# Three fused last layers: where the sparsemax threshold is subtracted, where int8 values are rounded, and in which step each piece runs

## The chip, the core and the metric

The kernel runs on one core of one Trainium2 chip. The metric is the time of the whole program on the device, in microseconds (us). The core has five instruction streams that matter here: TensorE (PE in the profile; PEld are its weight loads), VectorE (DVE), ScalarE (ACT), GpSimd (POOL) and SyncE (SP, which issues most DMAs). TensorE writes its products into PSUM banks; the other engines read them from there, except GpSimd, which in this kernel works on SBUF tiles only.

## What is computed

The program runs a stack of twelve layers over `x` (32 x 128 x 128). The change touches the last three, which the kernel calls `layer9`, `layer10` and `layer11`:

```python
# layer 9: 16 heads of width 8 attend to 32 patterns, with sparsemax in place of softmax
def sparsemax(z):
    z_sorted = -jnp.sort(-z, axis=-1)
    cum = jnp.cumsum(z_sorted, axis=-1)
    k = jnp.arange(1, S + 1, dtype=z.dtype)
    support = 1.0 + k * z_sorted > cum
    k_sup = jnp.sum(support, axis=-1, keepdims=True)
    tau = (jnp.take_along_axis(cum, k_sup - 1, axis=-1) - 1.0) / k_sup
    return jnp.maximum(z - tau, 0.0)
A = sparsemax(scale * scores)
x = x + (einsum('bhls,bshd->blhd', A, values).reshape(B, L, H * D) @ Wo + bo)

# layer 10: softmax attention to a context, probabilities times a dropout mask
# layer 11: each row scaled by its largest absolute value / 127, rounded to int8,
#           multiplied by int8 weights, scaled back, plus a bias
x_scale = jnp.maximum(amax, EPS) / 127.0
x_q = jnp.clip(jnp.round(x2d / x_scale), -128, 127).astype(jnp.int8)
```

Every layer is preceded by a layer norm and adds its result to `x`.

## The kernel before

The 4096 rows of `x` stay in SBUF as eight groups of 512 rows (`G` = 8), each a tile of 128 partitions by `J` = 4 blocks by 128 columns. The last three layers run as one software pipeline in `layer9` (line 1928).

**What a group goes through.** `scores` norms a group, projects it and puts its 128 x 2048 scores z (4 blocks x 16 heads x 32 patterns) into a `gbig` tile. `sort` sorts each run of 32 scores in 15 stages; a stage is two VectorE instructions (a max and a min) on tiles called `bbig`, and ten of the stages have two ScalarE copies of the elements that the stage leaves alone. `attend` works on four chunks c of 128 columns (4 heads each). `turn_top(c)` turns the sorted scores over on TensorE and ScalarE moves them to SBUF. `lower(c)` makes the candidate thresholds by products with the constant `means`; VectorE takes the largest as `tau`, and GpSimd subtracts it from z in place. `turn_z(c)` turns z over by four TensorE transposes into a `ps` bank, from which ScalarE takes max(z, 0) (a Relu) to SBUF; `value(c)` multiplies that by the value matrix `vb` into 32 rows of an `acc` bank. Then the result is turned back, projected and added. `layer10` and `layer11` follow, each a generator whose `yield`s cut it into steps.

**What sets the order.** Line 2087 builds a schedule by hand: rounds i = 0 to 10 of 15 slots n = 0 to 14. In slot n of round i comes stage n of the sort of group i, and then one step each of `layer11` (group i - 3), `attend` (group i - 1), `layer10` (groups i - 2 and i - 1), `scores` (group i + 1) and `layer11` (group i - 2), in that order, where the numbers behind the name list slot n. In the first slots pieces of the layer before are mixed in.

`follow(T, A, V)` forces TensorE, ScalarE and VectorE to run their instructions in exactly the order in which the program names them, for rounds 0 to 7. So within these engines an instruction that waits holds up all that stands behind it. GpSimd and the DMA queue are ordered by the tile scheduler, and so are all engines in the three last rounds, after `follow()`, where nothing is sorted any more; these are called the tail below.

The buffers that the change concerns: two PSUM banks `ps`, two `acc`, five SBUF tiles `bmid`, ten `gmid`, and four small tiles of 4 x 4 numbers for `tau`. In `layer11`, `E` is GpSimd for groups 0 to 6 and VectorE for group 7.

Of the kernel before, what the change touches and what calls it, by code (L numbers as in the profile page):

```python
# [11 lines left out]
BF16 = mybir.dt.bfloat16  # L12
# [3 lines left out]
ALU = mybir.AluOpType  # L16
AX = mybir.AxisListType
# [7 lines left out]
J = 4  # L25
# [5 lines left out]
class Columns:  # L31
# [5 lines left out]
    def add(self, name, a):  # L37
        a = np.asarray(a)
        assert a.ndim == 2 and a.shape[0] <= 128, (name, a.shape)
        self.at[name] = (a.shape[0], self.n, a.shape[1])  # L40
        self.parts.append(a)
        self.n += a.shape[1]
# [161 lines left out]
def program(ctx, tc, cols, x, ctxt, mask, drop, dfirst, dsmall, dwide, drows, dunits, dexperts, dconst, drel, dwq, out):  # L204
# [29 lines left out]
    def gmid(shape=(128, 512), dtype=F32):  # L234
        return mid.tile(list(shape), dtype, tag="gmid", name="gmid", bufs=10)

    def bmid(shape=(128, 512)):
        return mid.tile(list(shape), F32, tag="bmid", name="bmid", bufs=5)
# [19 lines left out]
    def bc(ap, axis, n):  # L258

        ap = ap.unsqueeze(axis)  # L260
        shape = list(ap.shape)
        shape[axis] = n
        return ap.to_broadcast(shape)
# [1664 lines left out]
    def layer9():  # L1928
# [55 lines left out]

        def attend(i):

            z, top, sTs, aTs = zs[i], ordered[i], {}, {}

            def turn_top(c):
                t = ps()  # L1990
                for j in range(J):
                    T.transpose(t[:, j * 128 : (j + 1) * 128], top[:, j * 512 + c * 128 : j * 512 + c * 128 + 128], ident)
                sTs[c] = bmid()
                A.activation(sTs[c], t, AF.Identity, bias=K["minus"])

            def lower(c):
                tau, m, sT = small(J, 4), acc((128, J, 4, 32)), sTs.pop(c)
                for j in range(J):
                    mm(m[:, j].rearrange("p h k -> p (h k)"), sT[:, j * 128 : (j + 1) * 128], K["means"])
                V.tensor_reduce(tau, m, AX.X, ALU.max)  # L2000
                part = z[:, :, c * 128 : c * 128 + 128].rearrange("p j (h k) -> p j h k", k=32)
                P.tensor_tensor(part, part, bc(tau, 3, 32), ALU.subtract)

            def turn_z(c):
                t = ps()
                for j in range(J):
                    T.transpose(t[:, j * 128 : (j + 1) * 128], z[:, j, c * 128 : (c + 1) * 128], ident)
                aTs[c] = bmid()
                A.activation(aTs[c], t, AF.Relu)

            def value(c):
                mm(yT_ps[32 * c : 32 * c + 32, :], vb[:, c].rearrange("p h e -> p (h e)"), aTs.pop(c))

            turn_top(0)
            turn_top(1)
            yield
            lower(0)
            lower(1)
            turn_top(2)
            yield  # L2020
            lower(2)
            turn_top(3)
            yield
            lower(3)
            turn_z(0)
            yield
            yT_ps = acc()
            for c in range(3):
                value(c)
                turn_z(c + 1)  # L2030
                yield
            value(3)
            yT = gmid()
            A.copy(yT, yT_ps)
            yield

            by = yT.rearrange("p (n l) -> p l n", l=16)
            rows = gbig((32, 16, 16, 8))
            for c in range(0, 4, 2):
                t = two((32, 8, 128))  # L2040
                for n in range(8):
                    T.transpose(t[:, n, :], by[:, 4 * c + n, :], ident)
                A.copy(rows[:, :, 4 * c : 4 * c + 8, :], t.rearrange("p l (h e) -> p h l e", h=16))
                yield
            t = ps((128, 16, J, 8))
            for h in range(16):
                T.transpose(t[:, h].rearrange("p j l -> p (j l)"), rows[:, h].rearrange("p l e -> p (l e)"), ident[0:32, 0:32])
            yT = gmid((128, J, 16, 8))
            for j in range(J):
                A.copy(yT[:, j], t[:, :, j])  # L2050
            yield
            zs.pop(i), ordered.pop(i)
            project(i, yT.rearrange("p j h l -> p (j h l)"), W["a3_Wo"], None)
            yield
# [33 lines left out]
        for i in range(G + 3):  # L2088
            for n in range(15):
                todo = []  # L2090
                add = lambda f, g, *at: todo.extend((f, g) for a in at if a == n and 0 <= g < G)
                add(layer11, i - 3, 0)
                add(attend, i - 1, 0, 1, 2, 3, 4, 5, 6, 7, 8, 9, 10, 11)
                add(layer10, i - 2, 0, 1, 2, 3, 5, 6, 7)
                add(layer10, i - 1, 12, 14)
                add(scores, i + 1, 4, 6, 7, 8, 11, 12)
                add(layer11, i - 2, 8, 10, 11, 12, 14)
                schedule.append((i, n, todo))
        for slot, (i, n, todo) in enumerate(schedule):
            if slot == G * 15:  # L2100
# [29 lines left out]
    def layer10(i):  # L2130

        E = P if i < G - 1 else V
        c, dm = load_ctx(i), gmid((128, J, D))
        SY.dma_start(out=dm, in_=drop[i * J : i * J + J].rearrange("b q k -> q b k"))
        steps = norm_turned(i, WW["L3_xattn_bout"])
        next(steps)
        yield
        next(steps)
        yield
        xnT = next(steps)  # L2140
        yield
        s = ps((128, J, 128))
        for j in range(J):
            cols_j = slice(j * 128, (j + 1) * 128)
            mm(s[:, j, :], xnT[:, cols_j], ctxT[i][:, cols_j])
        m, den, rec = small(J), small(J), small(J)
        pr = bmid((128, J, 128))
        V.tensor_reduce(m, s, AX.X, ALU.max)
        V.tensor_scalar(m, m, -1.0 / 32, None, ALU.mult)
        yield  # L2150
        for half in range(2):
            for j in (2 * half, 2 * half + 1):
                A.activation(pr[:, j], s[:, j], AF.Exp, bias=m[:, j : j + 1], scale=1.0 / 32, accum_out=den[:, j : j + 1])
            if half == 1:
                E.tensor_tensor(pr, pr, dm, ALU.mult)
                V.reciprocal(rec, den)
            yield
        prT = bmid()
        transposed(pr, prT, A.copy)
        yield  # L2160
        o = ps()
        for j in range(J):
            cols_j = slice(j * 128, (j + 1) * 128)
            mm(o[:, cols_j], c[:, j, :], prT[:, cols_j])
        yT = gmid()
        A.copy(yT, o)
        yield
        p = ps((128, J, 128))
        for j in range(J):
            mm(p[:, j, :], yT[:, j * 128 : (j + 1) * 128], W["x3_W"])  # L2170
        for j in range(J):
            V.scalar_tensor_tensor(xg[i][:, j, :], p[:, j, :], rec[:, j : j + 1], xg[i][:, j, :], ALU.mult, ALU.add)
        yield


    def layer11(i):

        rnd = 1.5 * 2.0**23
        E = P if i < G - 1 else V
        xn = mid.tile([128, J, D], F32, tag="xn", name="xn", bufs=2)  # L2180
        steps = norm_act(xg[i], xn)
        next(steps)
        yield
        next(steps)
        P.tensor_tensor(xg[i], xg[i], bc(WW["qbias"], 1, J), ALU.add)
        yield
        am, inv = small(J), small(J)
        V.tensor_reduce(am, xn, AX.X, ALU.max, apply_absolute_value=True)
        V.tensor_scalar(am, am, 1e-6, 1.0 / 127.0, ALU.max, ALU.mult)
        V.reciprocal(inv, am)  # L2190
        yield
        q, qb = bmid((128, J, D)), gmid((128, J, D), BF16)
        for j in range(J):
            A.mul(q[:, j, :], xn[:, j, :], inv[:, j : j + 1])
        E.tensor_scalar(q, q, 127.0, -128.0, ALU.min, ALU.max)
        E.tensor_scalar(qb, q, rnd, rnd, ALU.add, ALU.subtract)
        yield
        t = ps((128, 512), BF16)
        for j in range(J):
            T.transpose(t[:, j * 128 : (j + 1) * 128], qb[:, j, :], identb)  # L2200
        qT = gmid((128, 512), BF16)
        A.copy(qT, t)
        yield
        p = ps((128, J, 128))
        o = bmid((128, J, D))
        for j in range(J):
            mm(p[:, j, :], qT[:, j * 128 : (j + 1) * 128], wq)
        for j in range(J):
            V.scalar_tensor_tensor(o[:, j, :], p[:, j, :], am[:, j : j + 1], WW["qscale"], ALU.mult, ALU.mult)
        V.tensor_tensor(xg[i], xg[i], o, ALU.add)  # L2210
        SY.dma_start(out=out[i * J : i * J + J].rearrange("b s d -> s b d"), in_=xg[i])
        yield
# [52 lines left out]
```

## Time and profile before

| | |
|---|---|
| time, median of 3 runs | 2817.82 us (2806.86 to 2824.95) |
| the profiled execution: its time, its span | 2813.02 us, 2811.2 us |
| busy: PE, DVE, ACT, POOL | 87%, 74%, 54%, 33% of the span |
| mean granted TensorE clock | 0.939 of full speed |

All operations are recorded by one helper, so nearly all carry the line L192; instructions are told apart by the names of what they write and read. `bbig<-bbig` on DVE is the sort; `gbig<-gbig,s` on POOL the subtraction of the threshold; `ps<-cs,gbig` with 128*128 on PE the turning over of z; `bmid<-ps` on ACT the Relu; `acc<-bmid,vb` on PE the value product; `gmid<-bmid` on POOL the rounding.

A PE row gives as 128*32 the weights' rows and columns, then the shape of what streams past them. A float32 product is recorded as two instructions; a float32 transpose as one.

The rounds can be found by the first stage of each sort, the only one that reads a `gbig` tile. Rounds 0 to 7 begin at 2350.2, 2403.2, 2454.6, 2508.7, 2556.6, 2604.4, 2652.0 and 2699.7 us, and the last sort ends at 2744.0. So rounds 3 to 6, in which all three layers run and nothing of the layer before is left, take 47.6 to 47.9 us each, and the tail from 2744 to the end 67 us.

### The profile page before, as it was taken

How to read it: one execution, taken by the hardware profiler on the slowest of the kernel's cores; microseconds unless marked ns; L12 is line 12 of the kernel's file. 1: busy time of each engine (PE TensorE's matmuls, PEld its weight loads, DVE VectorE, ACT ScalarE, POOL GpSimd, SP SyncE). 2: the span in 40 equal slices, each digit the busy share in tenths (PEclk: the TensorE clock that was granted, in tenths of full speed). 3: DMA queues.
4: the chain of work that ended last, by engine and by line, in shares of the span. 5: the costliest groups of instructions: out<-in, count | busy, mean ns of one | idle time of the engine just before them, and what ended most of it. 6: DMA issues, size and time to landing. Idle time of an engine off the chain costs nothing.

```text
span 2811.2 us, 56423 instructions
## 1 busy us (share of the span) xinstructions
PE 2449.9 (87%) x22993; PEld 1590.9 (57%) x23012; DVE 2076.9 (74%) x4091; ACT 1512.4 (54%) x3394; POOL 931.5 (33%) x969
## 2 busy tenths in 40 slices
PE   5998989999979999999997999988878999867664
PEld 3666667777744446666663444445555588444443
DVE  6898768878888858788886454557897525889993
ACT  4665544444412247777773444457885324556663
POOL 3454442322301123445541000133441354243432
PEclk8898899999999999999999999999999999988886
DMA  3000000000000010000000000000002358000000
GB/s 119 2 3 2 6 21 9 9 5 4 14 12 0 1 34 2 6 10 13 10 2 16 1 0 1 1 1 1 2 13 78 103 187 258 16 23 12 23 12 19
DMA packets 51045, 73.77 MB, mean 26 GB/s; under 512 B 3905, under 2 KB 41538, under 8 KB 50658
## 3 DMA queue, kind: packets, MB, share of 16 engines
q1 hardware_dynamic: 47728, 61.63, 7.0%
q0 software_dynamic: 2624, 5.40, 0.5%
q8 instruction: 181, 2.97, 0.4%
q10 hardware_dynamic: 434, 3.14, 0.3%
q14 instruction: 78, 0.64, 0.1%
HBM read 57.26 MB, written 12.89 MB: 25 GB/s over the span
## 4 chain that ended last, share of the span: by engine, by line
PE 55%; DVE 28%; ACT 8%; issue 3%; POOL 2%; DMA 2%; SPq 0%; DVEq 0%; ACTq 0%; POOLq 0%
PE ps L192 23%; PE two L192 17%; PE acc L192 15%; DVE bbig L192 11%; DVE s L192 8%; ACT bbig L192 4%; DVE gmid L192 4%; DVE bmid L192 3%; ACT bmid L192 1%; POOL xn L192 1%; ACT gmid L192 1%; DMA ys<-yt,at 1%; DVE x L192 1%; ACT xn L192 1%; POOL s L192 1%
## 5 line engine op out<-in xcount | busy, mean ns | idle before, releaser
L192 PE MATMUL ps<-cs,bbig 128*128 128x128 f32 x2208 | 334.4, 289 | 86.2 <-ACT bbig L192 32.8
L192 PEld LDWEIGHTS ps<-cs,bbig 128*128 128x128 f32 x2208 | 248.7, 145 | 198.1 <-ACT bbig L192 94.5
L192 ACT COPY bbig<-ps 128x512 f32<-128x512 f32 x418 | 227.2, 583 | 187.1 <-PE ps L192 186.9
L192 DVE TENSOR_REDUCE s<-two 128x8 f32<-128x1024 f32 (+1 forms) x192 | 234.1, 1220 | 72.7 <-PE two L192 71.5
L192 PE MATMUL two<-xnT,u 128*128 128x512 f32 x512 | 262.4, 614 | 12.1 <-ACT bmid L192 5.5
L192 DVE TENSOR_TENSOR bbig<-bbig 128x1024 f32<-128x1024 f32 (+3 forms) x234 | 248.0, 1100 | 9.4 <-ACT bbig L192 7.7
L192 PE MATMUL acc<-bmid,u 128*128 128x512 f32 x416 | 220.2, 616 | 10.2 <-DVE bmid L192 8.9
L192 DVE TENSOR_TENSOR bmid<-bmid,ps 128x512 f32<-128x512 f32 x192 | 130.0, 683 | 114.2 <-ACT bmid L192 94.7
L192 ACT ACTIVATE bbig<-two,s 128x256 f32<-128x256 f32 (+1 forms) x512 | 189.8, 419 | 21.2 <-DVE s L192 17.5
L192 POOL TENSOR_SCALAR gbig<-bmid,cs 128x512 f32<-128x512 f32 x96 | 148.5, 1563 | 149.4 <-ACT bmid L192 149.3
L192 PE MATMUL two<-gbig,gmid 32*128 32x512 f32 (+1 forms) x1248 | 184.2, 564 | 0.0
L192 POOL TENSOR_TENSOR s<-s,cs 128x4 f32<-128x4 f32 x112 | 128.4, 1147 | 168.0 <-DVE s L192 163.0
L192 ACT ACTIVATE bbig<-bbig 128x512 f32<-128x512 f32 (+1 forms) x160 | 128.2, 801 | 68.2 <-DVE bbig L192 67.8
L192 PEld LDWEIGHTS two<-xnT,u 128*128 128x128 f32 x512 | 92.8, 193 | 116.8 <-issue 55.3
L192 ACT ACTIVATE bmid<-two 128x512 f32<-128x512 f32 x92 | 54.9, 597 | 171.8 <-PE two L192 163.9
L192 ACT ACTIVATE bmid<-two,ws 128x512 f32<-128x512 f32 x128 | 85.1, 686 | 114.5 <-PE two L192 114.3
L192 POOL TENSOR_TENSOR x<-x,xn 128x512 f32<-128x512 f32 x24 | 32.8, 1368 | 310.9 <-DVE xn L192 285.3
L192 PEld LDWEIGHTS acc<-bmid,u 128*128 128x128 f32 x416 | 76.9, 197 | 101.0 <-issue 48.2
L192 ACT ACTIVATE bbig<-bbig,s 128x128 f32<-128x128 f32 x384 | 118.8, 388 | 27.7 <-DVE s L192 27.7
L192 POOL TENSOR_TENSOR bbig<-bbig,s 128x1024 f32<-128x1024 f32 x32 | 60.6, 1893 | 213.3 <-PE two L192 152.7
L192 DVE TENSOR_TENSOR bbig<-two,s 128x512 f32<-128x512 f32 (+1 forms) x128 | 122.6, 958 | 8.6
L192 POOL TENSOR_SCALAR s<-s 128x4 f32<-128x4 f32 x60 | 14.0, 234 | 317.5 <-DVE s L192 317.4
(300 smaller groups left out, 5800.9 us busy)
## 6 DMA issues: line engine op xcount, KB each, us to landing
we<-in_experts SPq DMA_DIRECT2D x36, 768.0 KB
u<-in_units SPq DMA_DIRECT2D x9, 768.0 KB
gmid<-in_ctx SPq DMA_DIRECT2D x16, 256.0 KB
x<-in_x SPq DMA_DIRECT2D x8, 256.0 KB
gmid<-in_mask SPq DMA_DIRECT2D x8, 256.0 KB
ys<-bbig SPq DMA_DIRECT2D x2, 1024.0 KB
gmid<-ys SPq DMA_DIRECT2D x8, 256.0 KB
gmid<-in_drop SPq DMA_DIRECT2D x8, 256.0 KB
```

The costliest lines, as they stand in the source:

```text
L192: d = self.made = f(*args, **kwargs)
```

## The change

The threshold isn't subtracted in place by GpSimd any more. `lower` leaves the negated threshold in a small tile; `turn_z` makes, for each of the four blocks, an ordinary product of z with the identity matrix (instead of a transpose) and adds, by four further products whose weights are the threshold's column repeated 32 times, minus the threshold to the 32 rows of each head in the same bank. In `layer11` the clipped float32 values are turned over, and VectorE rounds them as it moves them from the PSUM bank to a bfloat16 tile; before, GpSimd rounded them to bfloat16, TensorE turned these over and ScalarE copied them. `layer10` and `layer11` get one more `yield` each, and the slots of `layer10`, `layer11` and `scores` are listed anew.

```diff
-                V.tensor_reduce(tau, m, AX.X, ALU.max)
-                part = z[:, :, c * 128 : c * 128 + 128].rearrange("p j (h k) -> p j h k", k=32)
-                P.tensor_tensor(part, part, bc(tau, 3, 32), ALU.subtract)
+                V.tensor_reduce(tau, m, AX.X, ALU.max, negate=True)
+                taus[c] = tau

             def turn_z(c):
                 t = ps()
                 for j in range(J):
-                    T.transpose(t[:, j * 128 : (j + 1) * 128], z[:, j, c * 128 : (c + 1) * 128], ident)
+                    cols_j = slice(j * 128, (j + 1) * 128)
+                    mm(t[:, cols_j], z[:, j, c * 128 : (c + 1) * 128], ident, True, False)
+                    for h in range(4):
+                        mm(t[32 * h : 32 * h + 32, cols_j], taus[c][:, j, h : h + 1].to_broadcast([128, 32]), ident, False, True)
                 aTs[c] = bmid()
                 A.activation(aTs[c], t, AF.Relu)
...
-                add(layer11, i - 3, 0)
+                add(layer11, i - 3, 0, 1)
                 add(attend, i - 1, 0, 1, 2, 3, 4, 5, 6, 7, 8, 9, 10, 11)
-                add(layer10, i - 2, 0, 1, 2, 3, 5, 6, 7)
+                add(layer10, i - 2, 0, 1, 2, 3, 4, 6, 7, 8)
                 add(layer10, i - 1, 12, 14)
-                add(scores, i + 1, 4, 6, 7, 8, 11, 12)
-                add(layer11, i - 2, 8, 10, 11, 12, 14)
+                add(scores, i + 1, 4, 6, 7, 8, 10, 12)
+                add(layer11, i - 2, 9, 10, 11, 13, 14)
...
         pr = bmid((128, J, 128))
+        yield
         V.tensor_reduce(m, s, AX.X, ALU.max)
...
-        q, qb = bmid((128, J, D)), gmid((128, J, D), BF16)
+        q = bmid((128, J, D))
         for j in range(J):
             A.mul(q[:, j, :], xn[:, j, :], inv[:, j : j + 1])
         E.tensor_scalar(q, q, 127.0, -128.0, ALU.min, ALU.max)
-        E.tensor_scalar(qb, q, rnd, rnd, ALU.add, ALU.subtract)
-        yield
-        t = ps((128, 512), BF16)
+        yield
+        t = ps()
         for j in range(J):
-            T.transpose(t[:, j * 128 : (j + 1) * 128], qb[:, j, :], identb)
+            T.transpose(t[:, j * 128 : (j + 1) * 128], q[:, j, :], ident)
         qT = gmid((128, 512), BF16)
-        A.copy(qT, t)
+        V.tensor_scalar(qT, t, rnd, rnd, ALU.add, ALU.subtract)
         yield
         p = ps((128, J, 128))
         o = bmid((128, J, D))
         for j in range(J):
             mm(p[:, j, :], qT[:, j * 128 : (j + 1) * 128], wq)
+        yield
         for j in range(J):
             V.scalar_tensor_tensor(o[:, j, :], p[:, j, :], am[:, j : j + 1], WW["qscale"], ALU.mult, ALU.mult)
```

More of the change, by code (lines that the diff above doesn't have):

```diff
@@ L1985, in attend @@
         def attend(i):
-            z, top, sTs, aTs = zs[i], ordered[i], {}, {}
+            z, top, sTs, aTs, taus = zs[i], ordered[i], {}, {}, {}
             def turn_top(c):
```

## The prediction

> **What bounds the kernel now.** The page as a whole is led by TensorE (87% busy), but the change acts after 2350 us only, so I read the stages of that part first: the busy time of each engine in a full round (from one first sort stage to the next) and in the tail. The columns are the stretch, its length, then PE, PEld, DVE, ACT and POOL busy, the granted clock and the DMA share.
>
> ```profile
> 2651.97:2699.70 47.73, 33.17 (x166) 21.67 (x166) 43.03 (x82) 29.86 (x67) 20.45 (x14) 0.82 0.06 17
> 2744.06:2811.20 67.14, 32.98 (x196) 25.55 (x196) 21.24 (x74) 25.25 (x64) 16.01 (x14) 0.65 0.07 20
> ```
>
> In a round VectorE works 43.0 of 47.7 us: it sets the pace. TensorE is idle for 14.6 us. In the tail nobody is near full: a chain of dependent steps sets it. Next, who VectorE waits for, in the round from 2608.56:
>
> ```profile
> DVE bbig L192 <- ACT bbig L192: 1.6, 3, 0.7
> DVE x L192 <- PE ps L192: 0.9, 1, 0.9
> DVE s L192 <- PE ps L192: 0.6, 1, 0.6
> DVE bmid L192 <- PE ps L192: 0.6, 1, 0.6
> DVE s L192 <- PE acc L192: 0.2, 1, 0.2
> ```
>
> None of its waits is for POOL, and all waits together are about 4 us. So the change can win at most 4.7 us a round, and only by taking VectorE's waits away or lightening its work. Then the timeline of one pass through `turn_z` and `value` (start, duration, engine):
>
> ```profile
> 2664.98 0.60 PE L192 MATMUL ps<-cs,gbig 128*128 128x128 f32 x4
> 2666.32 1.05 PE L192 MATMUL acc<-bmid,vb 128*32 128x512 f32 x2 [0.75 <-ACT bmid L192]
> 2667.30 0.66 PE L192 MATMUL ps<-cs,gbig 128*128 128x128 f32 x4
> ...
> 2669.68 0.66 PE L192 MATMUL ps<-cs,gbig 128*128 128x128 f32 x4
> ...
> 2672.69 0.60 ACT L192 ACTIVATE bmid<-ps 128x512 f32<-128x512 f32 x1 [1.25 <-PE ps L192]
> ...
> 2676.24 1.65 ACT L192 ACTIVATE xn<-x,s 128x128 f32<-128x128 f32 x4 [2.07 <-DVE s L192]
> 2677.80 1.12 ACT L192 COPY bbig<-bbig 128x512 f32<-128x512 f32 x2
> ```
>
> This is a serial loop, since T is held to program order: turn z (0.6), Relu (0.6), `value` (1.0), turn the next: 2.35 us a chunk. The last Relu ends at 2673.3. Behind it on ACT stand the norm of `scores` (1.65) and the two copies of sort stage 7 (1.12), without which VectorE can't start stage 8; that was at 2678.95. The loop has slack there: ACT waited 2.07 us for VectorE before the norm.
>
> **Turning z over, the main cost.** Today 4 instructions a chunk, 0.6 us. New, for each of 4 blocks: one full product (2 instructions) and four 32-column ones (8 instructions), 40 in all. The nearest row for the narrow ones is the weighted sum of layers 3, 4 and 7, with the same shape:
>
> ```profile
> 1994.17 1.08 PE L192 MATMUL acc<-bbig,val 128*32 128x128 f32 x32
> 1995.07 1.06 PE L192 MATMUL acc<-bbig,cs 128*32 128x128 f32 x32
> 1996.05 1.16 PE L192 MATMUL ps<-ws,gmid 128*128 128x128 f32 x8
> ```
>
> 32 narrow instructions take 1995.07 - 1994.17 = 0.90 us, 0.028 each: four run beside one another. Full ones take 0.11 each. A switch costs extra: from narrow to full 1996.05 - 1995.07 = 0.98 instead of 0.90, and the next eight full ones take 1.16 where eight elsewhere take 1.06 (the product of `xnT` with `ctxT`): 0.18. From full to narrow about 0.09: a 512-column product before 1994.17 began at 1993.65, 0.52 where its pace is 0.43. Here the kind changes twice a block. One block: 2 x 0.11 + 8 x 0.028 + 0.09 + 0.18 = 0.71; a chunk 4 x 0.71 = 2.9, and about 0.2 until the last product is out: 3.1 us, 2.5 more than now. Bounds: without any switching cost 4 x 0.445 + 0.2 = 2.0; if the narrow ones don't overlap, 40 x 0.117 (the pace of the eight 128*32 transposes of 1.04 us at 2682.63) + 0.2 = 4.9. I take 3.1, because its rows have the same shapes and the same clock (1.0 in these slots).
>
> The Trainium skill, "TensorEngine Tiling (Array Packing)", Key Properties, says that changing the tiling mode, not just the tile, drains TensorE; its overview gives up to 4x for 32 columns. The trace shows both (0.028 against 0.11; the switches). By the 4x alone a chunk is the 2.0 of the lower bound.
>
> **One round, followed through the queues.** From the first sort stage: (a) To the first `turn_z` now 2664.98 - 2651.97 = 13.0. It hangs on ACT's move of the last turned-over top behind the copies of stage 2, not on VectorE's small waits there (0.6 + 0.2 + 0.2 + 0.6 = 1.6, which the new `yield`s and slots mostly remove, by standing a sort stage between product and reader): 12.9. `layer11`'s product now holds one `ps` bank until its reader in slot 1, so the two `turn_top`s of slot 0 share the other; cover is the 4.6 us of two sort stages, and without it some 1 us. (b) First `turn_z` to the end of the last Relu: now 8.3; new 8.3 + 4 x 2.5 = 18.3. (c) From there to stage 8: now 5.65, set by VectorE; new it is ACT's queue: copy of `prT` 0.6, norm 1.65, copies 1.1, hand-overs 0.2: 3.5. (d) Stage 8 to the next round: now 20.75. Added: four scale-and-adds of `layer10` moved from slot 7 to 8, 1.1 and 0.7 for their product, which hangs on the same ACT queue; the rounding, 0.6 net (a DVE read of a 128x512 bank takes 0.69). Taken off: ACT waits before stages 13 and 14, about 1.2, and 0.55 by which stage 14's pair (2.85, against 2.31 in round 0) is longer beside the POOL rounding; the rest cancels. 21.3. Sum 12.9 + 18.3 + 3.5 + 21.3 = 56.0 against 47.7: +8.3.
>
> The same delay shows earlier: `layer10`'s second pair of exponentials moves to slot 4, behind the second Relu on ACT; VectorE's reciprocal of their sums waits for it in slot 4, with the norm statistics of `scores` and stages 5 to 7 queued behind. It is late by about 6 us there, inside the sum above.
>
> **What costs nothing or little.** POOL loses 6.6 (four subtractions) and 2.7 us a round of 20.5; it ended no VectorE wait. The transposes of q are float32 now, 4 x 0.11, like bfloat16's 0.61 for four; they run beside sort stage 14. ACT loses a 0.57 us copy. Moving `layer11`'s end to slot 1 delays its store and the two loads behind it on SP by 1 to 2 us; the loads are first read in the next round. `scores`' first wide products move ahead of `attend`'s projection on T (1.9 us); the projection waits 0.8 us for ACT's four copies anyway, and VectorE comes to its reader later in its round than now, because of (d); without that cover it costs 1 us.
>
> The subtractions' effect on VectorE is a gain that I leave out: stage 4's pair takes 2.64 us (870 + 1771 ns) in round 6 and 1.37 in round 0, but beside it runs the dropout multiply, which stays. At most 1.3 us a round.
>
> The skill's "SBUF — State Buffer", section "SBUF: two separate sides", says that VectorE and GpSimd share a port pair as an exclusive lock, for which the loser fully blocks; read so, all four subtractions could each have held VectorE up, 6.6 us, and a round would cost only 8.3 - 6.6 = 1.7 more. The rows of this trace show no more than the 1.3 of stage 4 beside GpSimd's two-input work.
>
> **The sum.** Rounds 3 to 7: 5 x 8.3 = 41.5. Rounds 1 and 2 hold pieces of the layer before, TensorE is busy 43.4 of 51.4 us in round 1, and 10 us are added to it: between 2 and 10, I take 7 each, 14. Tail: the last group's loop +10, less since the order is free there and the subtraction (1.05) and POOL's rounding (1.94, on the chain) leave it: +5. Together +60 on the profiled 2813: 2873. The median lies 4.8 above the profiled run, so I say 2875.
>
> **Rivals.** *The switch is cheap* (2.0 a chunk): 4 x 1.1 less a round, +3.9; 5 x 3.9 + 2 x 3 + 1 = +26: 2839. For it: nothing here switches as often, and a queue of alternating loads may be filled ahead. *The narrow products run one by one* (4.9): +15.5 a round; 5 x 15.5 + 2 x 14 + 12 = +117: 2930. For it: in the trace overlap shows in long runs only. *The loop is hidden*, the one that is not slower: TensorE's 14.6 idle us swallow 4 x 2.5 and VectorE stays the bound with fewer waits and less POOL beside it. With today's 0.6 a chunk the path above is 46.0, -1.7 a round, seven rounds and 2 of the tail: 2799; with all VectorE waits gone 43.0: 7 x 4.7 + 3 = 36: 2777. It decides from 3.1 - 8.3/4 = 1.0 us a chunk downward, below even my lower bound; against it, the idle time lies in other slots than the loop. *The change does less than it says* is not likely: POOL's rows must vanish.
>
> **Numbers.** Less than 1% (28 us) can't be told from no change. Main case, 2846 to 2905: 0.58. Cheap switch, 2810 to 2846: 0.14. One by one, above 2905: 0.10. Hidden: 0.18, of which 0.10 below 2790. So faster 0.10, same 0.22, slower 0.68. The range 2810 to 2920 leaves out most of the hidden case and the end of the dear one, about 0.18.
>
> **What would show it.** Right: `ps` rows with `s` as weights, 128*32, some 1024 of them; 3 us from a chunk's first product to its Relu; rounds of 55 to 57 us with VectorE's busy time unchanged near 43 and waits for ACT of about 5 us before its reciprocal and before stage 8. Wrong: rounds at 48 us or less, or VectorE waiting elsewhere, on the projection or the bank that is held in slot 0.

## The result, and the profile after

| | before | after |
|---|---|---|
| time, median of 4 runs each | 2812.55 us (2806.86 to 2824.95) | 2887.07 us (2879.80 to 2891.38) |
| ratio, 95% interval | | 1.0271 [1.0248, 1.0295] |
| the profiled execution: its time, its span | 2813.02 us, 2811.2 us | 2891.38 us, 2889.6 us |
| mean granted TensorE clock | 0.939 | 0.940 |

The change costs 2.7%: 74.5 us by the medians, 78.4 by the two spans. The forecast was 2875, some 60 more than before. The same stretches as before, a full round and the tail, by the busy time of each engine (stretch, length, then PE, PEld, DVE, ACT, POOL, granted clock, DMA share):

```profile
2702.80:2760.10 57.30, 41.65 (x310) 27.13 (x310) 43.50 (x83) 29.09 (x67) 12.03 (x8) 0.86 0.05 14
2814.03:2889.60 75.57, 44.35 (x340) 31.83 (x340) 22.85 (x77) 23.87 (x61) 9.98 (x9) 0.70 0.06 18
```

VectorE has the same work, 43.5 us, but the round grew from 47.7 to 57.3. GpSimd gave up 8.4 us of work and TensorE took on 8.5. Now VectorE is idle for 13.8 us of a round, and the list of its waits in this round (whom for, us in total, how many, the longest) says where:

```profile
DVE s L192 <- ACT bmid L192: 6.0, 1, 6.0
DVE bbig L192 <- ACT bbig L192: 4.9, 1, 4.9
DVE x L192 <- PE ps L192: 1.3, 2, 0.8
DVE s L192 <- PE acc L192: 0.7, 1, 0.7
DVE s L192 <- ACT xn L192: 0.4, 1, 0.4
```

Two waits for ScalarE make 10.9 of it. The timeline of TensorE (start, duration) shows what ScalarE itself waits for, one chunk of `turn_z` and its `value`:

```profile
2716.39 0.39 PE L192 MATMUL ps<-cs,gbig 128*128 128x128 f32 x2
2716.70 0.42 PE L192 MATMUL ps<-cs,s 128*32 128x128 f32 x8
2717.06 0.49 PE L192 MATMUL ps<-cs,gbig 128*128 128x128 f32 x2
...
2719.02 0.42 PE L192 MATMUL ps<-cs,s 128*32 128x128 f32 x8
2720.23 1.05 PE L192 MATMUL acc<-bmid,vb 128*32 128x512 f32 x2 [0.78 <-ACT bmid L192]
2721.20 0.49 PE L192 MATMUL ps<-cs,gbig 128*128 128x128 f32 x2
```

A block takes 2717.06 - 2716.39 = 0.67 at first and 0.77 where both switches are in it; the next chunk begins 4.81 us after this one, where before it was 2.32. ScalarE's timeline gives the four Relus and what stands behind them, VectorE's the two waits:

```profile
2719.58 0.60 ACT L192 ACTIVATE bmid<-ps 128x512 f32<-128x512 f32 x1 [4.24 <-PE ps L192]
...
2734.14 0.60 ACT L192 ACTIVATE bmid<-ps 128x512 f32<-128x512 f32 x1 [4.26 <-PE ps L192]
2734.70 0.59 ACT L192 COPY bmid<-ps 128x512 f32<-128x512 f32 x1
2735.18 1.65 ACT L192 ACTIVATE xn<-x,s 128x128 f32<-128x128 f32 x4
2736.73 1.12 ACT L192 COPY bbig<-bbig 128x512 f32<-128x512 f32 x2
```

```profile
2725.76 0.18 DVE L192 RECIPROCAL s<-s 128x4 f32<-128x4 f32 x1 [6.02 <-ACT bmid L192]
...
2737.89 1.97 DVE L192 TENSOR_TENSOR bbig<-bbig 128x768 f32<-128x768 f32 x2 [4.90 <-ACT bbig L192]
```

From the last Relu (its end 2734.74) ScalarE works without a gap to the copies of stage 7, and 0.04 us after their end VectorE begins stage 8. So the loop product, Relu, value, product sets the pace of this stretch; VectorE stands still beside it.

By the round's four parts (round 6; the forecast in brackets): to the first `turn_z` 13.6 (12.9), from there to the end of the last Relu 18.4 (18.3), to stage 8 3.15 (3.5), to the next round 22.2 (21.3). Rounds 3 to 7 became 9.3, 8.9, 9.7, 9.6 and 9.6 us longer, 47.1 together (41.5); rounds 1 and 2 12.3 and 7.4 (7 each); the tail 8.4 (5). The rest, 3 us, lies ahead of round 0, where both programs are the same; over all traces of this document round 0 begins between 2344.0 and 2357.0 us, so that much is chance.

### The profile page after: what moved, and what is told of

Read it like the earlier page. It is cut to its first block, busy times and chain, and to the rows that moved or that the text cites. A ratio compares the mean times of both kernels' runs of the same rounds, so it can differ in the third digit from the quotient of the medians.

```text
span 2889.6 us, 58658 instructions
## 1 busy us (share of the span) xinstructions
PE 2530.4 (88%) x24145; PEld 1643.6 (57%) x24164; DVE 2076.0 (72%) x4098; ACT 1507.5 (52%) x3386; POOL 871.7 (30%) x930
## 4 chain that ended last, share of the span: by engine, by line
PE 59%; DVE 26%; ACT 8%; issue 3%; POOL 2%; DMA 1%; SPq 0%; ACTq 0%; DVEq 0%; POOLq 0%
PE ps L192 26%; PE two L192 16%; PE acc L192 16%; DVE bbig L192 9%; DVE s L192 8%; ACT bbig L192 4%; DVE gmid L192 4%; DVE bmid L192 3%; ACT bmid L192 2%; POOL xn L192 1%; DVE x L192 1%; POOL s L192 1%; ACT gmid L192 1%; ACT xn L192 1%; ACT gbig L192 0%
## 5 line engine op out<-in xcount | busy, mean ns | idle before, releaser
L192 DVE TENSOR_REDUCE s<-two 128x8 f32<-128x1024 f32 (+1 forms) x192 | 234.0, 1219 | 72.8 <-PE two L192 71.5
L192 PE MATMUL two<-xnT,u 128*128 128x512 f32 x512 | 260.0, 609 | 12.1 <-ACT bmid L192 5.6
L192 DVE TENSOR_TENSOR bbig<-bbig 128x1024 f32<-128x1024 f32 (+3 forms) x234 | 241.2, 1071 | 38.6 <-ACT bbig L192 36.9
L192 POOL TENSOR_TENSOR x<-x,ww 128x512 f32<-128x512 f32 x56 | 81.9, 1462 | 114.5 <-ACT xn L192 111.8
```

What stands on the lines that cost most here:

```text
L192: d = self.made = f(*args, **kwargs)
```

## The experiments

The table gives all runs. Part (a) is from the first sort stage to the first `turn_z`, (b) from there to the end of the last Relu, (c) to stage 8, (d) to the next round, all of round 6; "round" is the mean of rounds 3 to 6. Medians and ratios are of several runs, each ratio to runs of the kernel before on the same chip; rounds, parts and tail are of the one profiled execution, which for e2 lies 12 us above the median.

| kernel | median us | ratio to before, 95% | round | a | b | c | d | tail |
|---|---|---|---|---|---|---|---|---|
| before | 2812.6 | | 47.7 | 13.0 | 8.3 | 5.7 | 20.8 | 67.2 |
| changed | 2887.1 | 1.0271 [1.0248, 1.0295] | 57.1 | 13.6 | 18.4 | 3.2 | 22.2 | 75.5 |
| e1 subtraction only | 2880.7 | 1.0252 [1.0214, 1.0289] | 55.0 | 13.5 | 18.4 | 3.7 | 19.2 | 77.8 |
| e2 all but the subtraction | 2821.4 | 1.0034 [1.0012, 1.0055] | 50.8 | 13.1 | 8.3 | 5.3 | 24.5 | 66.3 |
| e3 changed, narrow ones last | 2858.2 | 1.0158 [1.0115, 1.0201] | 52.7 | 13.3 | 14.4 | 3.2 | 21.9 | 72.0 |
| e4 changed, late reciprocal | 2888.9 | 1.0272 [1.0236, 1.0308] | 57.3 | 14.0 | 18.4 | 3.2 | 21.7 | 75.9 |
| e5 slots only | 2838.2 | 1.0081 [1.0064, 1.0098] | 53.8 | 16.2 | 8.2 | 5.4 | 24.8 | 69.1 |
| e6 rounding only | 2806.5 | 0.9975 [0.9956, 0.9995] | 47.4 | 12.1 | 8.9 | 5.9 | 20.9 | 65.1 |
| e7 subtraction, narrow ones last | 2848.7 | 1.0123 [1.0101, 1.0146] | 50.9 | 13.9 | 14.4 | 3.7 | 19.2 | 72.9 |
| e8 e7, next chunk ahead of value | 2839.1 | 1.0080 [1.0059, 1.0100] | 49.2 | 14.1 | 12.0 | 4.5 | 19.4 | 72.4 |
| e9 e6, statistics early | 2808.2 | 0.9982 [0.9968, 0.9996] | 46.1 | 13.0 | 8.3 | 5.7 | 19.4 | 65.0 |
| e10 e6, multiply late | 2808.7 | 0.9988 [0.9973, 1.0003] | 46.1 | 12.3 | 9.2 | 4.5 | 19.5 | 64.7 |
| e11 e10, last chunk on TensorE | 2809.7 | 0.9981 [0.9966, 0.9996] | 45.9 | 12.1 | 10.8 | 3.7 | 19.3 | 67.1 |
| e12 changed, staggered | 2879.0 | 1.0240 [1.0205, 1.0276] | 54.7 | 13.3 | 17.0 | 3.2 | 21.2 | 74.7 |

### Which part of the change costs the time

The theory was that the longer loop is the cost; the rival, that the new places of the steps, or the rounding, are. e1 takes the subtraction alone into the kernel before, e2 takes it out of the changed one:

```diff
...
-                P.tensor_tensor(part, part, bc(tau, 3, 32), ALU.subtract)
+                V.tensor_reduce(tau, m, AX.X, ALU.max, negate=True)
+                taus[c] = tau
...
-                    T.transpose(t[:, j * 128 : (j + 1) * 128], z[:, j, c * 128 : (c + 1) * 128], ident)
+                    cols_j = slice(j * 128, (j + 1) * 128)
+                    mm(t[:, cols_j], z[:, j, c * 128 : (c + 1) * 128], ident, True, False)
+                    for h in range(4):
+                        mm(t[32 * h : 32 * h + 32, cols_j], taus[c][:, j, h : h + 1].to_broadcast([128, 32]), ident, False, True)
```

In e2 the same lines of the changed kernel are turned back; the rounding by VectorE, the two yields and the slots stay.

> The kernel before with one part of the change alone: the threshold is subtracted by TensorE in turn_z; rounding, yields and slots are those of before. Theory (the longer turn_z loop is the whole cost): a chunk takes 3.06 us from its first product to its Relu as in the changed kernel, rounds 3 to 7 take 55 to 58 us, and the time is 2870 to 2895 us. Rival (the new places of the steps and the rounding by VectorE cost the time): rounds within 2 us of the 47.7 of before, time 2800 to 2830.

> The changed kernel with GpSimd's subtraction and the four plain transposes put back; the rounding by VectorE, the two yields and the new slots stay. Theory (loop): rounds of 46 to 48 us as on the path with 0.6 us a chunk, time 2795 to 2812 us, that is 0 to 17 below before. Rival (placement or rounding at fault): rounds above 52 us and a time over 2850.

e1's time came out as the theory said, 2880.7: +68.6 on its runs of before, 92% of the whole change; its rounds 3 to 7 take 53.8 to 55.4 us, at the lower end of 55 to 58 or just below. e2 came between the two: neither 0 to 17 us below before nor over 2850, but 9 us above before, with rounds of 50.8. So the loop is the main cost, and the rest of the change is not the small gain that the theory expected of it. The windows of e2's round 6 in the four parts show where it is lost (three of them are given):

```profile
2683.00:2691.40 8.40, 6.06 (x29) 2.60 (x27) 8.37 (x18) 5.86 (x17) 5.05 (x4) 1.00 0.01 3
2691.40:2696.70 5.30, 3.45 (x14) 1.66 (x14) 3.73 (x6) 3.15 (x8) 0.96 (x1) 1.00 0.00 0
2696.70:2721.20 24.50, 13.79 (x62) 8.77 (x62) 20.29 (x44) 13.54 (x34) 5.77 (x5) 0.74 0.00 0
```

The loop is back at 8.3 us (the window of 8.40 holds it) and VectorE works through it (8.37). But part (d), 24.5 us, has only 20.3 of VectorE's work in it, and its timeline names the waits, all behind steps that were moved:

```profile
2700.15 1.12 DVE L192 SCALAR_TENSOR_TENSOR x<-ps,s,x 128x128 f32<-128x128 f32 x4 [1.46 <-PE ps L192]
...
2709.65 0.69 DVE L192 TENSOR_TENSOR x<-x,ps 128x512 f32<-128x512 f32 x1 [1.48 <-PE ps L192]
2711.35 0.69 DVE L192 TENSOR_REDUCE s<-xn 128x4 f32<-128x512 f32 x1 [1.01 <-ACT xn L192]
```

These are `layer10`'s scale-and-adds, the add of `attend`'s projection and `layer11`'s maximum. In the changed kernel's round 6 the same three waits are 0.52, 0.80 and 0.36. It would be natural to say that there the long loop makes VectorE late and so covers them. But e2's own round 3, with the same order of steps and as short a loop (8.3 us), hardly has them; its part (d) as a window, and the same three rows:

```profile
2545.82:2567.00 21.18, 10.50 (x62) 6.92 (x62) 20.20 (x43) 13.51 (x34) 5.76 (x5) 0.87 0.00 0
2548.31 1.13 DVE L192 SCALAR_TENSOR_TENSOR x<-ps,s,x 128x128 f32<-128x128 f32 x4 [0.52 <-PE ps L192]
2556.26 0.68 DVE L192 TENSOR_TENSOR x<-x,ps 128x512 f32<-128x512 f32 x1
2557.16 0.69 DVE L192 TENSOR_REDUCE s<-xn 128x4 f32<-128x512 f32 x1 [0.22 <-ACT xn L192]
```

The work is the same (20.2 us of VectorE), the part 3.3 us shorter, and the granted clock 0.87 instead of 0.74: the waits come with the low clock, in which TensorE makes those products late (62 matmul records take 10.5 us in the one, 13.8 in the other). So what the rest of the change costs depends on where the clock is low; no run sets the clock by itself, and why it is low in rounds 4 to 6 of e2 stays open. e2's ten times, 2811.1 to 2833.5 us, fit: at 2811 the mean clock was 0.941 and 0.943, at 2833 it was 0.935 and 0.936.

e5 and e6 split the rest. e5 is the kernel before with the two yields and the new slots:

```diff
-                add(layer10, i - 2, 0, 1, 2, 3, 5, 6, 7)
+                add(layer10, i - 2, 0, 1, 2, 3, 4, 6, 7, 8)
...
```

e6 is the kernel before with VectorE's rounding:

```diff
-        E.tensor_scalar(qb, q, rnd, rnd, ALU.add, ALU.subtract)
...
-        A.copy(qT, t)
+        V.tensor_scalar(qT, t, rnd, rnd, ALU.add, ALU.subtract)
```

> The kernel before with the two yields and the new slots alone; GpSimd still subtracts and rounds. Rounds 4 to 7 took 51 to 52 us with new slots and VectorE rounding together, 47.7 before. Theory A (the new slots carry the difference: what they put behind one another waits): rounds of 50 to 52 us, new waits of 1 to 1.5 us before layer10's scale-and-adds and before the add of attend's projection, time 2815 to 2828 us. Theory B (VectorE's rounding carries it): rounds of 47 to 48.5 us, time 2803 to 2813.

> The kernel before with VectorE's rounding alone; slots and subtraction as before. Theory A (slots carry the difference): VectorE gets 0.6 us more a round and stage 14 about 0.5 us back, so rounds of 47 to 48.5 us and a time of 2805 to 2818 us. Theory B (rounding carries it): rounds of 50 to 52 us, 2818 to 2830.

Theory A holds in kind, and e5 lies above both of its ranges: slots alone cost 6.1 us a round and 23 in all, and the two waits are 2.2 and 1.7 us, not 1 to 1.5. Rounding alone gains 0.25%; the trace shows 2.1 us of it in the tail (65.1 against 67.2), where POOL's rounding was on the chain. e5 is worse than e2 because the new slots don't fit GpSimd's rounding. TensorE's timeline at the start of its round:

```profile
2667.45 0.61 PE L192 MATMUL ps<-identb,gmid 128*128 128x128 bf16 x4 [9.62 <-POOL gmid L192]
```

The turning over of q is named ahead of the sorted scores; with POOL's 2.7 us of rounding before it, TensorE stands for 9.6 us, works at a granted clock of 0.50 for the 10.6 us that follow (window 2667.4 to 2678.0), and part (a) takes 16.2.

### What makes a chunk 3 us long

In the changed kernel the kind of product switches from full to narrow four times a chunk. e3 makes the same 40 instructions with one switch; e7 does the same with the old slots and GpSimd's rounding; e12 puts each block's narrow products behind the next block's full one, since the narrow ones might also be slow for adding to columns that were just written.

```diff
-                for j in range(J):
-                    cols_j = slice(j * 128, (j + 1) * 128)
-                    mm(t[:, cols_j], z[:, j, c * 128 : (c + 1) * 128], ident, True, False)
-                    for h in range(4):
-                        mm(t[32 * h : 32 * h + 32, cols_j], taus[c][:, j, h : h + 1].to_broadcast([128, 32]), ident, False, True)
+                for j in range(J):
+                    mm(t[:, j * 128 : (j + 1) * 128], z[:, j, c * 128 : (c + 1) * 128], ident, j == 0, False)
+                for j in range(J):
+                    for h in range(4):
+                        mm(t[32 * h : 32 * h + 32, j * 128 : (j + 1) * 128], taus[c][:, j, h : h + 1].to_broadcast([128, 32]), ident, False, j == 3)
```

In e12 `full(j)` and `narrow(j)` stand for the two bodies above:

```diff
+                full(0)
+                for j in range(1, J):
+                    full(j)
+                    narrow(j - 1)
+                narrow(3)
```

> The changed kernel with the same 40 instructions of a chunk in another order: first the four full products of z, then the sixteen narrow ones with the threshold, so that the kind of product changes once a chunk and not four times. Theory (the switches between the kinds carry the chunk beyond 2.0 us): a chunk 8 x 0.11 + 0.09 + 32 x 0.028 + 0.2 = 2.1 us instead of 3.06, four chunks 4 us a round, seven rounds and the tail about 30: time 2850 to 2865. Rival (the number of products counts, not the switches): a chunk stays at 3.0 us and the time at 2880 to 2892.

> The kernel before with the threshold subtracted by TensorE, the four full products of z first and the sixteen narrow ones behind them; rounding and slots of before. A chunk takes 2.2 us there instead of 3.06, 3.5 us a round less. Theory (the loop is on the path whole): round 6 falls from 54.8 to 51.3 us, time 2846 to 2860. Rival (with the old slots VectorE sets the pace once the chunk is short): 48 to 49 us a round, 2818 to 2832.

> The changed kernel with the narrow products of each block moved behind the full product of the next block, so that no narrow product adds to columns that were written just before it; the kind changes from full to narrow three times a chunk and back twice, where the changed kernel has four and three, and the kernel with all narrow ones last has one and none. From a chunk's first product to its Relu the last two take 3.19 and 2.19 us, 0.33 us a change there and back. Theory (the changes of kind cost it): 2.19 + 2 x 0.33 = 2.86 us a chunk, 1.3 us a round less than the changed kernel, time 2874 to 2884. Rival (adding to columns that are just being written costs it): 2.2 to 2.3 us a chunk as with all narrow ones last, time 2850 to 2864.

TensorE's timeline, first of e3, then of e12, one chunk each:

```profile
2690.25 1.06 PE L192 MATMUL ps<-cs,gbig 128*128 128x128 f32 x8
2691.23 1.08 PE L192 MATMUL ps<-cs,s 128*32 128x128 f32 x32
2693.09 1.04 PE L192 MATMUL acc<-bmid,vb 128*32 128x512 f32 x2 [0.78 <-ACT bmid L192]
2694.07 1.16 PE L192 MATMUL ps<-cs,gbig 128*128 128x128 f32 x8
```

```profile
2707.86 0.61 PE L192 MATMUL ps<-cs,gbig 128*128 128x128 f32 x4
2708.40 0.43 PE L192 MATMUL ps<-cs,s 128*32 128x128 f32 x8
2708.75 0.49 PE L192 MATMUL ps<-cs,gbig 128*128 128x128 f32 x2
2709.17 0.42 PE L192 MATMUL ps<-cs,s 128*32 128x128 f32 x8
2709.53 0.49 PE L192 MATMUL ps<-cs,gbig 128*128 128x128 f32 x2
2709.94 0.64 PE L192 MATMUL ps<-cs,s 128*32 128x128 f32 x16
```

From the first product to the Relu: 3.19 us in the changed kernel (four switches to narrow, three back; 3.06, the figure in the first expectations, is to the end of the last product), 2.85 in e12 (three and two; the Relu began at 2710.71), 2.19 in e3 (one and none; 2692.44). A straight line: 0.33 us for each switch there and back, in these three orders, whatever columns are added to. e12's chunk is the theory's 2.86, and the rival's 2.2 to 2.3 is excluded; e3's and e7's times, too, lie in the theory's ranges. The chunk is on the path whole: e3's shorter loop gives 4.0 us in part (b) and 4.4 in the round, e7's 4.0 in (b) and 4.1 in the round against e1. e12's round fell by 2.4 (1.3 expected), 1.3 of it in (b). The 1.0 in (d) is not the products' order but the clock. TensorE's rows of the next group's scores and `attend`'s projection (`ps<-ws,gmid`), first in the changed kernel's round 6, then in e12's:

```profile
2744.63 3.01 PE L192 MATMUL two<-kb,gmid 128*128 128x512 f32 x4
2747.43 1.75 PE L192 MATMUL ps<-ws,gmid 128*128 128x128 f32 x8
```

```profile
2734.76 1.98 PE L192 MATMUL two<-kb,gmid 128*128 128x512 f32 x4
2736.59 1.05 PE L192 MATMUL ps<-ws,gmid 128*128 128x128 f32 x8
```

From 2745.5 to 2748.9 the changed kernel's granted clock is 0.50, and the projection's reader waits 0.80 us; in e12 it does not wait. The changed kernel's own round 4, without this stretch, has a part (d) of 21.2 us like e12. e12's time lies where expected.

e8 names the next chunk's `turn_z` ahead of `value`, so that TensorE does not stand while ScalarE makes the Relu:

```diff
             for c in range(3):
-                value(c)
                 turn_z(c + 1)
+                value(c)
                 yield
```

> As the kernel with old slots and the narrow products last, and in addition the next chunk's turn_z is named before the value product of the chunk before it, so that TensorE turns over one chunk while ScalarE makes the Relu of the other. Theory (the loop is serial through product, Relu and value): cadence 3.1 to 3.2 us a chunk instead of 3.86, 2 to 3 us a round less than without, time 2825 to 2845. Rival (one of the two ps banks is held by layer10's scores, so the next chunk cannot start ahead): no difference from the kernel without, within 6 us.

The time lies in the theory's range (2839.1) and beyond the rival's 6 us, but the round falls by 1.7, less than the 2 to 3 expected. The four chunks begin 2.8, 2.9 and 3.4 us apart, part (b) falls from 14.4 to 12.0. The first step is as the rival had it: chunk 1's products wait 0.78 us and start when the Relu of chunk 0 is done (2685.11 against 2685.06); from there to the last `value` TensorE works without a gap. This shape is still 0.8% slower than before: (b) and (c) together take 16.5 us instead of 14.0. That the twenty products of a chunk are too long for the slack of 2 us, even with one switch and hardly any waiting, fits this.

### Are VectorE's two waits one?

```diff
                 E.tensor_tensor(pr, pr, dm, ALU.mult)
-                V.reciprocal(rec, den)
...
             mm(p[:, j, :], yT[:, j * 128 : (j + 1) * 128], W["x3_W"])
+        V.reciprocal(rec, den)
```

> The changed kernel with one VectorE instruction, the reciprocal of layer10's sums, moved from slot 4 to just before its first reader in slot 8. Theory (its wait of 6.0 us for ScalarE and the wait of 4.9 us before stage 8 have one cause, ScalarE's queue behind the four Relus): the first wait goes, the one before stage 8 grows by nearly as much, and the time is 2875 to 2892. Rival (the reciprocal's wait adds to the other): about 6 us a round over six rounds less, 2845 to 2860.

VectorE's waits in e4's round 6:

```profile
DVE bbig L192 <- ACT bbig L192: 11.3, 3, 7.3
```

The 6.0 us before the reciprocal is gone, and the waits for ScalarE's copies are 11.3 instead of 4.9: 1.2 before stage 5, 2.7 before stage 6, 7.3 before stage 8. The sum is 10.9 in the changed kernel and 11.3 now, the time the same. It was one delay, and the reciprocal only the first to meet it.

### Taking turns with GpSimd

The forecast left out a gain of up to 1.3 us at stage 4, since the dropout multiply beside it stays. VectorE's instructions did get shorter: in the changed kernel the pair takes 681 + 681 ns. It takes both parts of the change: e1, without the subtractions but with the multiply in its old slot, has 1785 + 680, and e2, with the subtractions and the multiply moved, 677 + 1535. The round wins nothing by it, since VectorE then waits 6.0 us before the reciprocal. And stage 1 grew, from 1222 + 1219 to 2176 + 1214 ns. The timelines of VectorE and GpSimd, first before, then after:

```profile
2653.81 1.64 POOL L192 TENSOR_TENSOR x<-x,ww 128x512 f32<-128x512 f32 x1 [1.53 <-ACT xn L192]
2654.90 1.12 DVE L192 SCALAR_TENSOR_TENSOR bmid<-ps,s,ww 128x128 f32<-128x128 f32 x4 [0.58 <-PE ps L192]
...
2667.82 2.56 DVE L192 TENSOR_TENSOR bbig<-bbig 128x512 f32<-128x512 f32 x2
2668.11 1.73 POOL L192 TENSOR_TENSOR bmid<-bmid,gmid 128x512 f32<-128x512 f32 x1
```

```profile
2704.03 2.23 POOL L192 TENSOR_TENSOR x<-x,ww 128x512 f32<-128x512 f32 x1 [3.91 <-ACT xn L192]
2705.17 3.31 DVE L192 TENSOR_TENSOR bbig<-bbig 128x1024 f32<-128x1024 f32 x2
```

After, GpSimd's add (1.27 us when alone) starts while VectorE is in stage 0's second instruction, which ends at 2705.13, and it ends 1.13 us later, at 2706.26; VectorE's instruction of stage 1, 1.21 us when alone, starts at 2705.17 and ends 1.08 after the add. They run one after the other. Before, the same add met `layer11`'s scale-and-adds, which read a PSUM bank, and these kept their 1.12 us. The change moved them behind stage 1, and with them the cover. The Trainium skill, "SBUF — State Buffer", section "SBUF: two separate sides", says just this: a VectorE operation with two SBUF inputs and a GpSimd operation that reads SBUF hold their shared ports in turn, for the whole instruction. The rows agree with the rule; what it costs depends on what VectorE has beside it.

Three kernels try to win by it, on top of e6. e9 moves the norm statistics of `scores` between stages 3 and 4:

```diff
-                add(scores, i + 1, 4, 6, 7, 8, 11, 12)
+                add(scores, i + 1, 3, 6, 7, 8, 11, 12)
```

e10 moves the multiply, with the reciprocal placed as in e4:

```diff
-                add(layer10, i - 2, 0, 1, 2, 3, 5, 6, 7)
+                add(layer10, i - 2, 0, 1, 2, 4, 5, 6, 7)
```

e11 is e10 with chunk 3 by the lines of e3, and chunks 0 to 2 as before.

> The kernel before with VectorE's rounding, and the norm statistics of scores moved from slot 4 to slot 3, so that they stand between the threshold's maximum and sort stage 4. In the trace of before GpSimd's two-input operations and VectorE's pair of stage 4 wait for one another (870 + 1771 ns instead of 685 + 684). Theory (VectorE and GpSimd take turns when both read two SBUF tiles, and the statistics do not take part): stage 4's pair shrinks by 0.5 to 1.0 us as part of GpSimd's work runs beside the statistics; 3 to 6 us less than with the rounding alone, ratio to before 0.995 to 0.997. Rival (the delay only moves to the next stage): ratio as with the rounding alone, 0.9975 within 0.001.

> The kernel before with VectorE's rounding; layer10's second pair of exponentials and the dropout multiply behind them move from slot 3 to 4, and the reciprocal to just before its reader. Theory (taking turns): the multiply runs beside the norm statistics, as in the changed kernel; stage 4's pair, 2.6 us, is then delayed by the last subtraction alone and takes 2.0 to 2.3 us; 2 to 4 us less than with the rounding alone if the transposes of slot 5 do not wait for the multiply. Rival: they wait 1 to 2 us, TensorE's loop has 2.07 us of slack, so no change or up to 5 us more.

> As the kernel with the late multiply, and the last of the four chunks has its threshold subtracted by TensorE (four full products, then sixteen narrow ones), the other three by GpSimd. Theory: that chunk takes 1.6 us more, less than the loop's slack of 2.07 us, so it costs nothing, and stage 4's pair falls to 1.4 to 1.7 us as no two-input GpSimd work runs beside it: 5 to 9 us less than before in all, ratio 0.9965 to 0.9985 or lower. Rival (the loop is on the path already): 1 to 1.6 us a round more, ratio 1.000 to 1.003.

The rounds answered, the totals did not. GpSimd's subtractions reach into stage 3 in some rounds, so stages 3 and 4 have to be read together. In round 6 they take 1226 + 1230 and 870 + 1771 ns before, 1202 + 2065 and 1075 + 1533 in e6, 1243 + 1249 and 679 + 1531 in e9, 1267 + 1268 and 989 + 1532 in e10, 1217 + 2072 and 675 + 678 in e11: 5.1, 5.9, 4.7, 5.1 and 4.6 us. Stage 4's pair shrinks by 0.4 us in e9 (0.5 to 1.0 expected), is above the 2.0 to 2.3 expected in e10 (the last subtraction still runs in it, and the multiply now after it), and is 1.35 in e11, where stage 3 takes the delay in its place (in e11's rounds 4 and 5 stage 3 is not longer, and the pair takes 1.6, in the 1.4 to 1.7 expected). VectorE's and GpSimd's rows of e11:

```profile
2664.57 1.28 DVE L192 TENSOR_TENSOR bbig<-bbig 128x512 f32<-128x512 f32 x2
2665.77 0.86 DVE L192 BATCH_NORM_STATS2 s<-x 128x6 f32<-128x128 f32 x4
...
2666.00 1.29 POOL L192 TENSOR_TENSOR bmid<-bmid,gmid 128x512 f32<-128x512 f32 x1 [3.03 <-ACT bmid L192]
```

The multiply runs beside the norm statistics and neither is longer for it. The mean round fell from 47.4 to 46.1, 46.1 and 45.9, which is 5 to 6 us over four rounds. Not all of it is these moves: e6's own part (d) is 19.35 us in round 4, at a granted clock of 0.90, and 20.87 in round 6, at 0.75; e9's round 6 has 19.36 at 0.90.

The ratios, 0.9982, 0.9988 and 0.9981, are no better than e6's 0.9975, and all four intervals overlap. e9 misses its 0.995 to 0.997 and lies in its rival's range. e10 is as its rival said, no faster; the transposes of slot 5 waited 0.98 us for the multiply. e11 lies in its theory's range, 0.9965 to 0.9985, but so does e6 without any of it. For e11 the traces show where some goes: its tail is 2.0 us and its round 2 5.7 us longer than e6's; e10's round 2 is 2.4 longer. For e9 they show no such place, and runs of one kernel lie 15 to 20 us apart: what is left is below what these runs can tell. e6 has the lowest ratio of all, not clear of e9 to e11; e6, e9 and e11 beat the kernel before by 0.2%, and all three undo most or all of the subtraction on TensorE.

## Why the prediction was right, and where it was off

**The mechanism and the main term held.** A chunk was forecast at 3.1 us and took 3.19 to its Relu; part (b) 18.3 against 18.4. The switch was the term with the largest doubt; 0.09 one way and 0.18 back were read off the long runs of the earlier layers, and e3 and e12 price a pair of switches at 0.33. That the sum came out so close is luck: a pair is 0.06 dearer than forecast, and the chunk holds three switches back, not the four that the sum charges at 0.18; the two errors are 0.18 us each and cancel. The narrow products do run beside one another: a group of four starts every 0.11 us in the long runs of e3. So the two rivals on the chunk fall, 2.0 and 4.9.

**Part (c) and the two waits held.** 3.15 against 3.5, waits of 6.0 and 4.9 against "about 6" and "about 5", VectorE's work 43.5 against 43; e4 shows that the first is inside the sum, as was said.

**Parts (a) and (d) were 0.7 and 0.9 us too short: the forecast left TensorE's clock out of them.** It read the clock for the chunk alone. Part (a) as a window, in round 6 of before and in rounds 4, 5 and 6 of the changed kernel (the granted clock is the third figure from the end):

```profile
2651.97:2664.98 13.01, 9.92 (x69) 8.94 (x70) 11.28 (x19) 8.10 (x16) 4.00 (x4) 0.75 0.22 60
2588.76:2602.83 14.07, 11.38 (x65) 10.35 (x66) 13.12 (x18) 6.45 (x11) 2.23 (x1) 0.65 0.20 56
2645.51:2658.75 13.24, 10.50 (x65) 9.39 (x66) 12.78 (x18) 6.45 (x10) 2.23 (x1) 0.71 0.22 61
2702.79:2716.39 13.60, 10.85 (x65) 9.74 (x65) 12.79 (x18) 6.46 (x10) 2.23 (x1) 0.69 0.20 58
```

The lower the clock, the longer the part, within one kernel. Length times clock stays nearly the same: 9.8 us before and 9.7 in e1 (13.53 at 0.72), 9.1 to 9.4 in the changed kernel, 9.3 in e2 and e12 (13.08 at 0.71, 13.28 at 0.70). By this measure the change makes (a) a little shorter, as forecast, and the 0.6 us on top come from a clock that stays at one half for longer. The 0.96 us of stage 1 are not on this path: e1, which does not have them, takes 13.5 too. In (d) it is the same: 21.2 us, the forecast's 21.3, in round 4 (at 0.86), and 22.5 and 22.2 in rounds 5 and 6 (0.81 and 0.82), where the low stretch falls on `attend`'s projection. No run changes the clock alone, so this is read from the rounds and not tested, and why the clock is low where it is stays open. The errors of the parts make 1.3 us in round 6 and 1.1 in the mean of rounds 3 to 7: 47.1 instead of 41.5 in all. (The forecast's own terms for (d) add up to 21.4; it wrote 21.3.)

**Round 1 was mis-sized:** +12.3, above the bounds of 2 and 10. The upper bound was the loop alone. e1's round 1 is 10.4 longer, so it seems that all of the loop counts where TensorE has least room, and e2's is 1.9 longer for the other edits; together 12.3. Round 2 (+7.4) was right by luck: e1's is 11.5 longer, more than the whole change, so such sums of single executions prove little.

**The tail's deduction was half wrong.** +10 for the loop was right (e1: +10.6), and about 2 for POOL's rounding as well (e6: -2.1); but e1, which has the subtraction out of GpSimd too, shows neither its 1.05 us nor the some 2 us that the free order was to save, and +8.4 stands where +5 was said.

**The rival that ends faster had the wrong price.** "With today's 0.6 a chunk the path above is 46.0" put part (c) of a long loop beside (b) of a short one. e2 is the nearest run (GpSimd still subtracts there, and stage 4's pair takes 2.2 us instead of 1.4): (c) is 5.3, not 3.5, since VectorE and not ScalarE then ends it, and (d) 21.2 at best and 24.5 at the low clock, not 21.3. Its round 3, at the high clock, takes 48.9 us and rounds 4 to 6 51.1 to 51.9, all above the 47.7 of before. At 0.6 us a chunk the change loses 9 us by the medians instead of winning 14; a chunk between 0.6 and 1.0 us was not run. The parts do not simply add up either: subtraction alone costs 7.2 us a round, the rest alone 3.0, and together they cost 9.4.

**"Beside it runs the dropout multiply, which stays" failed as a reason.** It stays, but its exponentials now stand in slot 4 behind the second Relu, so it runs 6 us after the end of stage 4, where VectorE computes norm statistics. In the old slots (e1) the reason holds: 1.1 us of the 1.3 us of delay stay. In the changed kernel VectorE's work is 1.3 us less at stage 4 and 0.96 more at stage 1, and neither is seen in the round, as the loop sets its pace.

## What to carry to other kernels

Taking work off an engine that ends no wait wins at most what it holds up by sharing with another (here 1.3 us a round at stage 4); before giving it to another engine, follow the loop that it enters: here 6.6 us of GpSimd's spare time became 10 us in a serial chain of TensorE and ScalarE, with VectorE, the busy engine, waiting at its end. Group products by their shape: a switch between full and 32-column products and back costs as much as three full 128-column instructions, so a chunk with its sixteen small products behind the four large ones takes 2.2 us, and alternating 3.2. A rival in which the main delay is gone needs its own path worked out, part by part. And before a wait of half a microsecond behind TensorE is put down to a new order of steps, compare rounds of the same kernel: here the same part took 21.2 us at a granted clock of 0.87 and 24.5 at 0.74.

## What was not expected of the hardware

- VectorE and GpSimd ran strictly one after the other where both read two SBUF tiles (2176 ns for 1214, 2.23 us for 1.27), and without any loss where VectorE read PSUM or computed norm statistics.
- Four narrow products start within 0.02 us of one another, and the next four 0.13 us after them in a run of eight instructions, 0.11 later on in a long run; only the switch costs, 0.09 us more than the usual 0.11 from full to narrow, and on the way back 0.09 more to the first full instruction and 0.10 more to the second.
- After 9.6 us of idle TensorE in e5 the granted clock was 0.50 for the next 10.6 us: four transposes that take 0.66 us at full clock took 1.1.
- The granted clock differs from round to round of one execution, and stretches of the schedule follow it: part (a) of the changed kernel takes 13.24 us at 0.71, 13.60 at 0.69 and 14.07 at 0.65.
